# A sparse two-layer graph network on one core: node groups of 16, sums on sixteenths of the array, blocks in pairs, list comparisons on another engine

## The chip, the cores and the metric

The kernel runs on one core of a Trainium2 chip. A core has five engines with a queue of instructions each: TensorE (PE in the profile; its weight loads are listed apart as PEld), VectorE (DVE), ScalarE (ACT), GpSimd (POOL) and SyncE (SP). They work in parallel and wait for each other by semaphores. Any of them may start DMA transfers between DRAM and the on-chip memory; POOL can also start *indirect* ones, which fetch 128 rows of a table in DRAM by a list of 128 row numbers. The metric is the device time of one execution in microseconds (us), the median of several runs.

## The reference

Two graph layers, each behind a layer norm with relu and added to its input. There are 3327 nodes (padded to 3328, 26 blocks of 128) with 512 features. The adjacency matrix is sparse, and its entries fall with the product of the two nodes' numbers: the first nodes are hubs. Every node has itself as a neighbour.

```python
# layer 0
h = jnp.maximum(_layernorm(x), 0.0)
x = x + adj @ (relu(adj @ (h @ W1) + b1) @ W2) + b2          # hidden width 128
# layer 1, with the new x
h = jnp.maximum(_layernorm(x), 0.0)
type_sum = adj @ h                                           # adj_a and adj_b are the same matrix
attn_a = sigmoid(concat([type_sum, h]) @ Wa.T + ba)          # one number per node
attn_b = sigmoid(concat([type_sum, h]) @ Wb.T + bb)
hW = h @ W_sa
scores = (hW @ a_sa[:D])[:, None] + (hW @ a_sa[D:])[None, :]
e = where(adj != 0, exp(-leaky_relu(scores, 0.01)), 0.0)
x_a = (e / (e.sum(1) + 1e-5)) @ hW
x_b = adj @ (h @ W_gcnb) + b_gcnb
x = x + sigmoid(attn_a * x_a + attn_b * x_b)
```

In layer 1 the kernel first sums rows of h (once with the entries of adj, once with those of e) and multiplies with the weights afterwards.

## The kernel before

The adjacency lies transposed in DRAM (`adjT`, row = neighbour j, column = target node). `chunks` are 512 target columns; `back` is their order in the first product, from the last one to the first, which has 256.

*First product.* For each chunk PE adds up `acc_u` (L568) over 26 tiles of 128 neighbours, while DVE reduces the same tiles to `most` (L572): the largest magnitude in each group of `GW` = 32 target columns, so four groups to a block. From that `make_lists` (L433) writes, per group, the list of neighbours that have any entry in it. It works one chunk behind: `flag` says whether neighbour j touches a group, a scan counts them along j (`upto`), two small products on PE count across the partitions (`offset`), and then each list place is filled by comparison: DVE compares the place number with `offset` (L502, tile `at`), PE multiplies `at` with the counts (`p_list`, L513), DVE counts again (`past`, `jb`) and writes two tables of row numbers: `row_h` (which row of h) and `row_a` (which group of 32 entries of adjT). The generator is advanced by one step per tile of the next chunk. As soon as a list stands, POOL gathers its adjacency groups into `ae` (`gather_behind`, L216, one gather behind three of four products). Lists have room for `rooms[i]` columns of 64 places for each of the four groups; ten blocks (`OWN`) take their own 128 nodes by a plain load instead (`load_own`, L196, on ACT's queue).

*Second product.* `acc_g` (L825) is dense for the first 18 blocks of targets. The last two chunks, blocks 18 to 25, are summed by lists: POOL gathers rows of g, PE adds them up (`list_sums`, L784). `make_h1` (L639) makes the rows of layer 1, stores them to `h_dram`, and makes the logits that a node's own row gives (`own_logits`, L628; three blocks named in `LATE` and the blocks in `OWN` have them later). Block 0, the hubs, is dense in layer 1 too (`acc_hub`, L709).

*Gathered part.* Blocks 25 down to 1 are done by lists. `attend` (L917) gathers a block's rows of h into a ring of 16 tiles with two rows per partition (`pairs`), then DVE and ACT make e from the scores next to the adjacency entries in `ae`. `sums` (L968) multiplies (L981) on quarters of the array: 64 neighbours x (32 entries of adj and 32 of e) with 64 x 512 of the rows, into half of one of two PSUM banks. `copy_out` (L1052) takes the banks to `ty` on ACT, `turn` (L988) transposes (`ptt`, L995; copies `tyT`, L1010), and `weigh` (L1026) multiplies with the weights (`p_b`, L1035; `p_a`, L1042); `finish` (L875) does the rest and stores.

What sets the order: instructions of an engine run in the order of issue, and `queued` puts an instruction behind a named one of its engine. In each turn of the loop block i's scores are made, block i+2 is weighed, block i+1 turned, and block i's sums come last. POOL's order is the order in which the loop asks for gathers; `AE_PER` adjacency gathers of later blocks are asked for per block (`fetch_ae`, L912). The first gather of a block waits (`pace`, L208) until the sums of an earlier block have been done: `LEAD` = 3 blocks back for the last eight blocks, 4 for the others.

```python
    lead = LEAD[i < NB - 8]
    if k0 + k + q == extra[i] and len(combined) >= lead:
        pace(gathered[0], combined[-lead])
```

Of the kernel before, what the change touches and what calls it, by code (L numbers as in the profile page):

```python
# [9 lines left out]
F32 = mybir.dt.float32  # L10
# [10 lines left out]
GW = 32  # L21
NQ = P // GW
HALF = P // 2
ROW = 520
LEAD = 3, 4
# [13 lines left out]
LATE = 10, 11, 16  # L39

OWN = 1, 6, 7, 8, 12, 13, 14, 15, 17, 18


def list_rooms(n_blocks):

    rooms = [0, 8, 7, 6, 5, 5] + 6 * [4]
    return (rooms + n_blocks * [3])[:n_blocks]
# [3 lines left out]
def kernel(  # L51
# [35 lines left out]
    rooms = list_rooms(NB)  # L87
    extra = [int(i in OWN) for i in range(NB)]
    first = [2 * sum(rooms[:i]) for i in range(NB)]
    NL = 2 * sum(rooms)  # L90


# [21 lines left out]
    for _ in range(WAKE):  # L114
# [21 lines left out]
    ae = [  # L136
        kept([P, 2 * (r + extra[i]), 2 * GW], f"ae{i}") if r else None for i, r in enumerate(rooms)
    ]

    def segments(i):  # L140

        r = rooms[i] + extra[i]
        n = -(-r // SEG)
        cuts = [-(-r * k // n) for k in range(n + 1)]
        return list(zip(cuts, cuts[1:]))
    hubp = ctx.enter_context(tc.tile_pool(name="hubp", bufs=6))
# [26 lines left out]
    listed, fetched = set(), [0] * NB  # L173

    def gather_adj():

        order = []
        for n, (c0, w) in enumerate(back):
            order += range(c0 // P, (c0 + w) // P)[:: 1 if n < LISTED else -1]
        for i in order:  # L180
            if not i:
                continue
            r = rooms[i]
            for k0, k1 in segments(i):
                for q in range(2):
                    for k in range(max(k0, extra[i]), k1):
                        while (i, q) not in listed:
                            yield None
                        f = first[i] + q * r + k - extra[i]
                        fetched[i] += 1  # L190
                        yield gather(
                            ae[i][:, 2 * k0 + q * (k1 - k0) + k - k0, :GW], adj_groups,
                            row_a[:, f : f + 1], NP * NG - 1,
                        )

    def load_own(i):  # L196

        n = segments(i)[0][1]
        for h in range(2):
            rows = slice(i * P + h * HALF, i * P + (h + 1) * HALF)  # L200
            nc.scalar.dma_start(
                ae[i][h * HALF : (h + 1) * HALF, 0 : n + 1 : n, :GW],
                adjT[rows, rows].rearrange("j (q i) -> j q i", i=GW),
            )
# [54 lines left out]
    with (  # L259
# [109 lines left out]
        lower = kept0([P, 1], "lower", F32)  # L369
        place_row = kept0([P, max(rooms) * HALF], "place_row", F16)  # L370
# [3 lines left out]
        def make_constants():  # L374
# [4 lines left out]
            for h in range(2):  # L379
                nc.vector.memset(apart[h * HALF : (h + 1) * HALF, 2 * h : 2 * h + 2], 0.0)  # L380
# [6 lines left out]
            for t, op, base in ((before, ALU.is_gt, 0), (shift, ALU.is_equal, -1)):  # L387
# [7 lines left out]
            nc.vector.memset(lower, 1.0)  # L395
            nc.gpsimd.affine_select(
                lower, lower, pattern=[[0, 1]], compare_op=ALU.is_ge, fill=0.0, base=-HALF,
                channel_multiplier=1,
            )
            first_iota = nc.gpsimd.iota(  # L400
                place_row, pattern=[[1, max(rooms) * HALF]], base=0, channel_multiplier=0,
# [9 lines left out]
            for r in sorted(set(rooms[1:])):  # L411
                i0, n = rooms.index(r), rooms.count(r)
                cols = slice(first[i0], first[i0] + n * 2 * r)
                nc.gpsimd.memset(limit[:, NQ * i0 : NQ * (i0 + n)], float(r * HALF))
                nc.gpsimd.iota(
                    place_col[:, cols], pattern=[[0, 2 * n], [HALF, r]], base=0,
# [3 lines left out]
                    group_col[:, cols], pattern=[[NQ, n], [1, 2], [0, r]], base=NQ * i0,  # L420
# [3 lines left out]
            for t, by in ((place_col, -float(HALF)), (group_col, 2.0)):  # L424
                nc.vector.scalar_tensor_tensor(
                    t, lower.to_broadcast([P, NL]), by, t, op0=ALU.mult, op1=ALU.add
                )
            yield
            for t in ae[1:]:
                nc.gpsimd.memset(t[:, :, :GW], 0.0)  # L430
            behind.close()

        def make_lists(nth, most):  # L433
# [10 lines left out]
            for b in range(w // P):  # L444
                if extra[c0 // P + b]:
                    groups = slice(b * NQ, (b + 1) * NQ)
                    own = flag[:, groups, c0 // P + b]
                    nc.vector.tensor_tensor(own, own, apart, ALU.mult)
# [19 lines left out]
            nc.vector.tensor_copy(offset[:, :n], p_off[:, :n])  # L468
# [4 lines left out]

            step = steps[nth % 2]
            p_sh = bank(psB, f"p_sh_{c0}")
            nc.tensor.matmul(
                p_sh[:, : n * NB], shift, after[:, :n, :].rearrange(flat), start=True, stop=True
            )
            nc.vector.tensor_tensor(
                step[:, :n, :NB], p_sh[:, : n * NB].rearrange("p (b j) -> p b j", j=NB),  # L480
                upto[:, :n, :], ALU.add,
            )
            yield
            batches = []
            for i in range(c0 // P, (c0 + w) // P):
                for q in range(2 if rooms[i] else 0):
# [835 lines left out]
```

## Time and profile before

| what | us |
|---|---|
| median of three runs | 836.75 (829.47 and 842.9) |
| the profiled execution | 834.5 |
| its span | 832.8 |
| PE busy in the span | 735.6 |
| DVE busy | 506.0 |
| POOL busy | 461.1 |
| ACT busy | 194.5 |
| mean granted clock of PE | 0.94 |

Durations of single instructions come from the profiled execution; its span is the time from its first to its last instruction on the core, 1.7 less than what it was timed at. Busy times are sums over the span; the stages of this kernel use the engines in very different shares, so the windows of the span tell more than these sums. An entry such as `hr<-h_rows,row_h` names the tile written and the tiles read; buffer numbers are left out.

### The profile page before, as it was taken

Reading aid. Unit: us, or ns where it says so; the run is one execution under the profiler, and the core shown is the slowest. Engines: PE = TensorE matmul, PEld = TensorE weight load, DVE = VectorE, ACT = ScalarE, POOL = GpSimd, SP = SyncE. Lnnn points to the kernel's source line nnn. Section 1 sums busy time; section 2 is a strip of 40 time slices with the busy share of each in tenths; the row PEclk is TensorE's granted clock in tenths of the full one; section 3 lists DMA queues with packets and bytes.
Section 4 is the critical chain, followed back from the end, with each engine's and each line's share of the span. In section 5 each row is a group of like instructions: output and inputs, shape, how many; then the busy total and the mean of one; then the engine's idle time right before and its main releaser. Section 6 shows DMA issues by size and latency. Waiting matters only on the chain.

```text
span 832.8 us, 11907 instructions
## 1 busy us (share of the span) xinstructions
PE 735.6 (88%) x3595; PEld 404.5 (49%) x3595; DVE 506.0 (61%) x1625; ACT 194.5 (23%) x402; POOL 461.1 (55%) x490
## 2 busy tenths in 40 slices
PE   9999888989899771999899749967999999999995
PEld 7774333444543220444355236633656655665554
DVE  7778868898860611798987225523665557553552
ACT  7770000000000110354544002211212222221121
POOL 2201756766657776534456766674657666767500
PEclk9999989999999875999999969996999999999999
DMA  8788988988878844789994755664667877767510
GB/s 271 245 287 259 326 246 242 293 272 246 232 232 284 262 132 134 240 279 312 327 314 135 241 150 145 199 185 115 195 211 244 255 206 233 240 205 234 178 51 29
DMA packets 104889, 185.08 MB, mean 222 GB/s; under 512 B 18401, under 2 KB 35441, under 8 KB 104818
## 3 DMA queue, kind: packets, MB, share of 16 engines
q1 hardware_dynamic: 66544, 113.43, 41.8%
q0 software_dynamic: 23264, 57.64, 24.3%
q10 hardware_dynamic: 15010, 13.18, 4.9%
q8 instruction: 30, 0.49, 0.2%
q14 instruction: 41, 0.34, 0.1%
HBM read 162.29 MB, written 22.26 MB: 222 GB/s over the span
## 4 chain that ended last, share of the span: by engine, by line
PE 72%; DVE 7%; issue 6%; another core or an unknown queue 6%; DMA 5%; ACT 2%; POOL 1%; SPq 1%; DVEq 0%; ACTq 0%; POOLq 0%
PE acc_u L568 17%; PE acc L981 12%; PE p_b L1035 11%; PE p_a L1042 10%; PE acc_g L825 8%; PE pu L333 3%; PE ptt L995 3%; DMA a<-in_adjT_dram 2%; PE acc_hub L709 2%; PE px L663 2%; PE pt L325 1%; DMA xb<-in_x_dram 1%; PE acc_s L784 1%; DMA hr<-h_rows,row_h 1%
## 5 line engine op out<-in xcount | busy, mean ns | idle before, releaser
L166 POOL DMA_INDIRECT ae<-in_adjT_dram,row_a x194 | 202.6, 1044 | 181.8 <-DVE past L519 54.3
L568 PE MATMUL acc_u<-a,rows 128*128 128x512 f32 (+1 forms) x364 | 161.0, 583 | 0.5 <-DMA a<-in_adjT_dram 0.5
L166 POOL DMA_INDIRECT hr<-h_rows,row_h x120 | 122.7, 1022 | 62.5 <-issue 27.4
L825 PE MATMUL acc_g<-a,g 128*128 128x512 f32 (+1 forms) x260 | 117.1, 584 | 7.2 <-DMA a<-in_adjT_dram 6.8
L572 DVE TENSOR_REDUCE most<-a 128x16 f32<-128x512 f32 (+1 forms) x182 | 112.3, 638 | 11.6 <-issue 6.3
L1035 PE MATMUL p_b<-W_g_sb,tyT 128*128 128x257 f32 x416 | 99.3, 391 | 15.8 <-DVE tyT L1010 15.3
L1035 PEld LDWEIGHTS p_b<-W_g_sb,tyT 128*128 128x128 f32 x416 | 77.8, 192 | 46.5 <-DVE tyT L1010 15.6
L166 POOL DMA_INDIRECT rows<-h_rows,row_h x74 | 75.1, 1015 | 44.3 <-PE acc L981 20.9
L568 PEld LDWEIGHTS acc_u<-a,rows 128*128 128x128 f32 x364 | 67.2, 195 | 58.8 <-issue 56.0
L1042 PE MATMUL p_a<-W_sa_sb,tyT 128*128 128x512 f32 (+2 forms) x216 | 94.2, 577 | 0.2
L1010 DVE COPY tyT<-ptt 128x512 f32<-128x512 f32 x51 | 34.8, 685 | 87.0 <-PE p_a L1042 31.7
L825 PEld LDWEIGHTS acc_g<-a,g 128*128 128x128 f32 x260 | 50.0, 200 | 58.5 <-issue 44.9
L981 PE MATMUL acc<-hr,ae 64*64 64x512 f32 x480 | 68.3, 614 | 4.4 <-issue 4.0
L166 POOL DMA_INDIRECT g_row<-g_rows,row_h x48 | 49.0, 1021 | 20.9 <-issue 13.4
L1042 PEld LDWEIGHTS p_a<-W_sa_sb,tyT 128*128 128x128 f32 x216 | 40.7, 189 | 38.8 <-issue 36.9
L884 ACT ACTIVATE f<-f 128x2 f32<-128x2 f32 x26 | 5.3, 203 | 192.4 <-DVE f L883 97.2
L981 PEld LDWEIGHTS acc<-hr,ae 64*64 64x64 f32 x480 | 27.6, 136 | 33.6 <-issue 33.0
L343 ACT ACTIVATE gT<-acc_u,b_col 128x512 f32<-128x512 f32 (+1 forms) x7 | 4.6, 656 | 163.8 <-DMA a<-in_adjT_dram 90.9
L663 PE MATMUL px<-W_sb,sT 128*128 128x512 f32 x52 | 26.7, 650 | 15.4 <-ACT sT L799 12.0
L666 DVE TENSOR_TENSOR xb<-px,xb 128x512 f32<-128x512 f32 x26 | 17.3, 682 | 36.6 <-PE px L663 28.5
L981 PE MATMUL acc<-rows,ae 64*64 64x512 f32 x296 | 37.1, 593 | 2.5 <-issue 2.3
L623 DVE SCALAR_TENSOR_TENSOR junk<-rows,w_rows 128x512 bf16<-128x512 f32 x52 | 35.6, 684 | 3.2 <-ACT rows L244 1.1
(159 smaller groups left out, 945.2 us busy)
## 6 DMA issues: line engine op xcount, KB each, us to landing
a<-in_adjT_dram SPq DMA_DIRECT2D x286, 256.0 KB
h_rows<-rows SPq DMA_DIRECT2D x26, 260.0 KB
x<-in_x_dram SPq DMA_DIRECT2D x26, 256.0 KB
xb<-in_x_dram SPq DMA_DIRECT2D x26, 256.0 KB
x<-xb ACTq DMA_DIRECT2D x26, 256.0 KB
x1b<-x SPq DMA_DIRECT2D x26, 256.0 KB
out_dram<-va SPq DMA_DIRECT2D x25, 256.0 KB
ae<-in_adjT_dram,row_a POOLq DMA_INDIRECT x194
```

The costliest lines, as they stand in the source:

```text
L166: return nc.gpsimd.indirect_dma_start(out=dst, out_offset=None, in_=table, in_offset=bass.IndirectOffsetOnAxis(ap=rows, axis=0), bounds_ch ...
L333: nc.tensor.matmul(pu[:, :HID], hT[:, k, :], W1_sb[:, k, :], start=(k == 0), stop=(k == KD - 1))
L568: added = nc.tensor.matmul(acc[:, :w], u[j], a[:, :w], start=(j == 0), stop=(j == NB - 1))
L572: nc.vector.tensor_reduce(most[:, : w // GW, j], a[:, :w].rearrange("p (b i) -> p b i", i=GW), axis=AX.X, op=ALU.max, apply_absolute_value ...
L623: return nc.vector.scalar_tensor_tensor(junk, h, 1.0, w_rows[:, s, :], op0=ALU.mult, op1=ALU.mult, accum_out=into)
L663: last_row[2] = nc.tensor.matmul(px, sT[:, b * P : (b + 1) * P], W2_sb, start=True, stop=True)
L825: added = nc.tensor.matmul(acc[:, :w], g[j], a[:, n % per, :], start=(n == 0), stop=(n == NB - 1))
L981: added = nc.tensor.matmul(taken[i]["acc"][h][q * HALF : (q + 1) * HALF, :], both[half_p, q * n + k, :], taken[i][k0][k][half_p, q, :D], s ...
L995: moved = nc.tensor.transpose(pt[:, k * P : (k + 1) * P], ty[h][:, k * P : (k + 1) * P], ident)
L1010: last = nc.vector.tensor_copy(dst, src)
L1035: nc.tensor.matmul(p_b[n][:, :WH], tyT[:, k, 0, :], W_g_sb[:, k, n * WH : (n + 1) * WH], start=(k == 0), stop=(k == KD - 1),)
L1042: last = nc.tensor.matmul(p_a[:, c0:c1], tyT[:, k, 1, :], W_sa_sb[:, k, c0:c1], start=(k == 0), stop=(k == KD - 1),)
```

## The change

- Groups have 16 target columns instead of 32 (`GW`), eight to a block. A list of a group is shorter, and there are twice as many lists.
- Blocks are worked on in teams: block 1 alone, then (2, 3), (4, 5) up to (24, 25). A list column now has 128 places: 32 for each of the two blocks' two halves (64 for block 1's halves). Columns per team, times four for the groups: 5, 7, 5, 5, 4, 4, 4, 4, 3, 3, 3, 3, 3.
- `sums` multiplies on tiles of 32 x 32 (64 x 32 for block 1), 16 of them, into four banks.
- Each pair team takes both blocks' own nodes by plain loads: eight loads per team on ACT's queue for the adjacency, four per team on SP's for the rows of h; for the two listed chunks also loads of g. `OWN` is gone.
- The comparisons of `at` are ScalarE activations: a sigmoid with slope 200, which is 0 or 1 at whole numbers.
- `list_sums` copies the adjacency groups to block-diagonal tiles (`diag`, 16 copies on ACT), so that one product serves two halves of a block.
- The loop weighs two blocks per turn, with a turn of the next pair put between `p_b` and `p_a` of the second. `LEAD` is 2 teams. Own logits of nine blocks (`LATE`) are made in the gathered part, of all the others in `make_h1`.

```diff
-GW = 32
+GW = 16
-LEAD = 3, 4
+LEAD = 2
+STEEP = 200.0
-LATE = 10, 11, 16
-OWN = 1, 6, 7, 8, 12, 13, 14, 15, 17, 18
+LATE = 8, 10, 11, 12, 13, 14, 15, 16, 17
+def make_teams(n_blocks):
+    teams = [(1,)] + [(i, i + 1) for i in range(2, n_blocks, 2)]
+    rooms = [5, 7, 5, 5, 4, 4, 4, 4] + n_blocks * [3]
+    return teams, rooms[: len(teams)]
...
+    tall = [P // (2 * len(t)) for t in teams]
+    extra = [len(t) - 1 for t in teams]
+    def tiles_of(m):
+        return [
+            (slice(r * tall[m], (r + 1) * tall[m]), teams[m][r // 2], r % 2)
+            for r in range(P // tall[m])
+        ]
...
+    def load_own(m):
+        n = segments(m)[0][1]
+        for part, i, h in tiles_of(m):
+            for s in range(2):
+                nodes = own_rows(i, h, s)
+                nc.scalar.dma_start(
+                    ae[m][part, 2 * s * n : (2 * s + 1) * n + 1 : n, :GW],
+                    adjT[nodes, nodes].rearrange("j (q i) -> j q i", i=GW),
+                )
...
-                        nc.vector.tensor_scalar(
-                            at[:, k : k + r, h, :],
-                            place_row[:, : r * HALF].rearrange("p (k m) -> p k m", m=HALF),
-                            offset[:, b : b + 1], None, op0=ALU.is_ge,
+                    for part, i, h in tiles_of(m):
+                        b = group(i, h, q)
+                        nc.scalar.activation(
+                            at[:, k : k + r, part],
+                            place_row[:, : r * t].rearrange("p (k m) -> p k m", m=t),
+                            AF.Sigmoid, bias=offset[:, b : b + 1], scale=STEEP,
...
+                for m in teams_in(c0, w):
+                    if extra[m]:
+                        load_own(m)
...
+        def make_diag(ms):
+            for t, m in zip(diag, ms):
+                n = 4 * (rooms[m] + 1)
+                for part, i, h in tiles_of(m):
+                    nc.scalar.copy(t[part, :n, h * GW : (h + 1) * GW], ae[m][part, :, :GW])
...
-                    lead = LEAD[i < NB - 8]
-                    if k0 + k + q == extra[i] and len(combined) >= lead:
-                        pace(gathered[0], combined[-lead])
+                        if k0 + k + q == extra[m] and len(combined) >= LEAD:
+                            pace(gathered[0], combined[-LEAD])
...
             for k in range(n):
-                for q in range(2):
-                    for h in range(2):
-                        half_p = slice(h * HALF, (h + 1) * HALF)
+                for q in range(4):
+                    for r, (part, i, h) in enumerate(tiles_of(m)):
                         added = nc.tensor.matmul(
-                            taken[i]["acc"][h][q * HALF : (q + 1) * HALF, :],
-                            both[half_p, q * n + k, :], taken[i][k0][k][half_p, q, :D],
+                            taken[m]["acc"][r][q * QW : (q + 1) * QW, :],
+                            both[part, q * n + k, :], taken[m][k0][k][q][part, :D],
...
+        def next_turn(added):
+            i, ty, es = turning.pop(0)
+            with queued(added):
+                tyT, added, copied = turn(i, ty, False)
+            turned.append((i, tyT, es))
+            held.append(copied)
+            return added
...
+        def weigh_all(added):
+            while weighing:
+                final = len(weighing) == 1
+                added, end = weigh_one(added, next_turn if final and turning else None)
+                if turning:
+                    added = next_turn(added)
+                held.extend(end())
+            return added
+        for m in range(M - 1, 0, -1):
+            with queued(*held):
+                for seg in segments(m):
+                    made = attend(m, seg)
...
+            fetch_ae(2 * AE_PER)
+            held, turned = [], []
+            added = weigh_all(added)
             with queued(added):
-                for seg in segments(i):
-                    added = sums(i, seg)
+                for seg in segments(m):
+                    added = sums(m, seg)
             combined.append(added)
+            weighing = turned
+            turning, last = copy_team(m)
+            held.append(last)
```

## The prediction

> **What bounds the kernel now.** I read the page's first and fourth parts first.
>
> ```profile
> PE 735.6 (88%) x3595; PEld 404.5 (49%) x3595; DVE 506.0 (61%) x1625; ACT 194.5 (23%) x402; POOL 461.1 (55%) x490
> PE 72%; DVE 7%; issue 6%; another core or an unknown queue 6%; DMA 5%; ACT 2%; POOL 1%; SPq 1%; DVEq 0%; ACTq 0%; POOLq 0%
> ```
>
> TensorE looks like the bound and POOL half idle. That is an average over unlike stages, so next the windows: columns are the window, its length, busy us and count of PE, PEld, DVE, ACT, POOL, then granted clock, DMA share, GB/s.
>
> ```profile
> 0.00:63.00 63.00, 61.36 (x387) 47.99 (x388) 47.24 (x161) 46.40 (x105) 11.69 (x54) 1.00 0.82 267
> 63.00:235.00 172.00, 154.29 (x730) 74.67 (x729) 145.06 (x381) 4.86 (x8) 103.64 (x101) 0.95 0.86 261
> 235.00:452.00 217.00, 179.35 (x642) 82.89 (x642) 130.12 (x427) 64.93 (x114) 126.02 (x119) 0.90 0.75 243
> 452.00:577.00 125.00, 95.87 (x431) 51.56 (x430) 47.30 (x172) 19.89 (x47) 80.73 (x81) 0.86 0.59 177
> 577.00:757.00 180.00, 178.87 (x1034) 108.40 (x1034) 100.46 (x356) 42.69 (x94) 118.41 (x116) 1.00 0.73 223
> 757.00:832.80 75.80, 65.91 (x375) 38.99 (x374) 35.88 (x132) 15.75 (x36) 20.64 (x20) 0.97 0.35 110
> ```
>
> Row 1 is the normalization, row 2 the first adjacency product with the lists (DVE 145 of 172 is close behind PE), row 3 the second product, the hub and the rows of layer 1. From 452 to the end runs the gathered part, the one that the change rewrites. In row 5 PE never stops; row 4, the same work, is 29 us short of busy. The chain of waits shows one block of row 5:
>
> ```profile
> 597.04 3.49 PE acc L981 x30
> 600.53 3.67 PE p_b L1035 x16
> 604.20 3.43 PE p_a L1042 x8
> ```
>
> Block after block is 11.67 us: p_b 3.67, p_a 3.43, 1.1 for turn and small sums, and the sums of gathered rows (3.43 where a block has four columns). So PE sets the pace there. But POOL is not far: its timeline shows what a gather costs and what its pauses are.
>
> ```profile
> 538.89 1.00 POOL L166 DMA_INDIRECT hr<-h_rows,row_h  x1 [1.72 <-remote]
> 540.19 1.02 POOL L166 DMA_INDIRECT hr<-h_rows,row_h  x1 [0.30 <-issue]
> ...
> 568.93 0.99 POOL L166 DMA_INDIRECT ae<-in_adjT_dram,row_a  x1 [0.30 <-issue]
> 577.46 0.99 POOL L166 DMA_INDIRECT rows<-h_rows,row_h  x1 [7.54 <-PE acc L981]
> ```
>
> 1.00 busy and 0.30 to the next: one gather per 1.31 us at best, whatever it fetches. From 538.9 to 570.2 stand 24 without pause. In windows of one block's length:
>
> ```profile
> 538.80:550.60 11.80, 11.80 (x64) 7.20 (x63) 5.46 (x19) 2.67 (x6) 9.07 (x9) 1.00 0.66 197
> 550.60:562.40 11.80, 5.07 (x18) 2.15 (x16) 0.36 (x1) 1.34 (x3) 8.97 (x9) 0.86 0.67 188
> 562.40:574.20 11.80, 7.00 (x16) 1.75 (x19) 1.33 (x4) 0.00 (x0) 5.98 (x6) 0.50 0.43 119
> 577.40:589.20 11.80, 11.80 (x70) 7.22 (x70) 6.67 (x26) 2.18 (x7) 7.98 (x8) 1.00 0.59 183
> ```
>
> PE, DVE and ACT fall silent in the middle of the train and wake about 2 us after it. It isn't data: a copy of finished sums waits.
>
> ```profile
> 547.97 0.63 ACT L898 ACTIVATE va<-vb 128x512 f32<-128x512 f32 x1 [0.82 <-issue]
> 557.39 0.58 ACT L1054 COPY ty<-acc 128x512 f32<-128x512 f32 x1 [8.79 <-remote]
> ```
>
> Its sums had ended on PE at 546.9. Five trains have 12 gathers or more (90.5, 248.6, 302.4, 455.6, 538.9 us); in them PE, beyond its usual spacing, loses 3.9, 8.4, 21.6, 17.6 and 10.4 us. About thirty shorter ones (up to 9) lose 2 or nothing. So a long train without pause goes with a stop of the rest. The trace shows no cause, only that it starts with a dense burst of PE instructions inside the train.
>
> **The change, part by part.**
>
> *Sums.* Before: 428 matmuls of 64x64, two passes each, 856. How many run at once is read from the weight loads:
>
> ```profile
> 586.02 0.24 PEld L981 LDWEIGHTS acc<-hr,ae 64*64 64x64 f32 x4 [0.19 <-issue]
> 586.45 0.24 PEld L981 LDWEIGHTS acc<-hr,ae 64*64 64x64 f32 x4 [0.19 <-issue]
> ```
>
> Four per 0.43 us, 107 ns each: 856 x 0.107 = 92 us. After: 960 of 32x32 and 40 of 64x32 (block 1). If sixteen run at once: 1920/16 x 0.43 = 51.5, plus 80/8 x 0.43 = 4.3, 56 us: 36 us less PE. If only eight: 107, 15 more. Nearest row: p_list's 64-wide pairs are issued at 16 ns per load-and-matmul, under the 27 that sixteen per 0.43 need, so I take sixteen.
> The Trainium skill, "TensorE: Matmul & The Clock Gate", "Measured speedup vs the span model", gives 10.6 times for sixteen 32x32 tiles. The trace has four quarters at the full four times and no sixteenth. By the page the sums would take an estimated 26 us more than I count.
>
> *Gathers.* With groups of 16, lists are shorter but twice as many. POOL's order holds, from the first layer-1 gather on, 194 + 22 = 216 gathers before and 212 + 41 = 253 after (adjacency gathers 194 to 212, own-block columns not counted). 253 x 1.31 = 331 us, in a stage whose gathers now end at 785 (785 - 452 = 333). Per team of two blocks in the middle (three columns, 12 + 4 gathers) 21.0 us of POOL against 14.2 weighing + 2.3 turning + 3.4 sums = 19.9 of PE; with four columns 26.2 against 20.8; five 31.4 against 21.6; team 1 has 29 gathers, 38. **POOL becomes the bound of this stage.** PE's 36 us are then worth nothing: they become idle time of PE.
>
> *Pauses.* One gate per team (LEAD = 2) replaces one per block. The first 30 gathers come without one, then trains of 16 to 29, and, POOL being late, the gate is open when it gets there: no pause. Every train is of the long kind, and each team's sums are one burst of 128 matmuls. The rows for that are the five trains above. A burst inside a train either goes on (0) or waits for its end; I take the second, as four of the five lost 8 us or more. Then POOL and the burst take turns, since the next-but-one train is gated by the burst. Behind the gated gather on POOL's queue stand all later gathers, the adjacency ones of teams still ahead too; sums of the next team wait for them.
>
> *Banks.* A team's sums want four banks, the ones that its predecessors' turns just used. The second turn is put between p_b and p_a of a weighing, so its two copies (0.69 each) lie beside 3.43 of p_a: nothing. Without that cover 1.4 per team, 17 in all; the four copies of the sums (0.57 each) lie beside the next weighing.
>
> *List making.* 100 comparisons on DVE (L502, 300 ns at the common 128x192) go, -27 us there; scan, flag, step on twice the elements give back about 2.6 per chunk, 18. 200 ACT instructions at 0.3 (e_hub's exp, 128x128, 305 ns) = 60 us over six chunks on an engine that is idle in row 2 (4.86 of 172). PE gains 420 p_list matmuls at 16 ns, 7 us, and about 30 more switches between acc_u and p_list at about 0.1 to 0.2 (522 and 533 ns steps against 429): +9 to 11 on PE, 154 of 172 busy. Ahead of the comparisons on ACT's queue stand 16 loads of own blocks per chunk (96 in all, 20 before, 0.35 to 0.67 us each); once, at 96.57 to 104.07, an ACT issue was 7 us late. Between -10 (DVE was the wait) and +30 (each of six chunks 5 late); I take +8.
> *The rest.* Four blocks' own logits move from the gathered part into row 3 (+6.7 us of DVE, not always the bound there), and three from the lists' blocks; the train at 302 becomes 12 + 12, at best -20; 16 block copies and one or two more table loads (1.28 each) on ACT; SP's 48 small loads of own rows instead of 10 large ones, issued a team (over 20 us) ahead of their use. Between -25 and +10, I take -3. Sum ahead of 452: **+5**.
>
> **The sum**, against the profiled execution (span 832.8, 834.5 with what lies around it; the median of three runs is 836.75, within 0.3%). Gathered part: start 452; 30 gathers 39; sums of team 12 3.4; 203 gathers up to team 1's last 266; eleven bursts 41 (56 less 4.3, 3.4 and 6.9); twelve hand-overs at 0.5, 6; sums of team 1 6.9: 814. Tail: weigh 4 and 5 14.2, turn 2.2, sums 2.6, weigh 2 and 3 14.4, last sums 1.7, and from there as now (815.4 to 832.8) 17.4: 53. 867 + 5 = 872 of span, 874 in all: about 4.5% slower. Ten us up or down is the ring of 16 row pairs (a gather waiting for its tile) and the burst's length: own range 852 to 895.
>
> **Rivals.**
> 1. *Not slower: the long train doesn't stop the burst.* Then only POOL's count decides: 452 + 233 x 1.31 = 757, 13 for landing, scores and team 1's sums, 53: 823 + 5 + 2 = **830** (815 to 850). For it: trains of 8 lose nothing, and nothing in the trace names the cause. Against: five of five long ones lost. It decides if PE's bursts pass at 0.43 us per sixteen inside a train of 16; then the changed kernel's page shows PE busy through the trains.
> 2. *Slower still: sixteenths run eight at once.* In the turn-taking sum 48 of 51 us count: **922**. Speaks for it: weight loads as many as matmuls; against: the 16 ns above.
> 3. *Lists late*: the ACT queue holds p_list by 5 us per chunk; **900**.
> 4. *Faster: long trains are harmless now in the first 452 us as well* (21.6 of the train at 302, or all 34 of three): 830 - 20 to -35: **795 to 812**.
>
> **Chances.** Forecast 0.42, rival 1 0.28 (a sixth of it under 820), rival 2 0.10, rival 3 0.08, rival 4 0.12. A change under 2% (820 to 853) can't be told from none. Faster 0.12 + 0.05 = 0.17; same 0.23 of rival 1 and 0.03 of the forecast, 0.26; slower 0.57. The range leaves out half of rival 4 and most of rival 2: 812 to 915.
>
> **What would show it.** POOL about 1.31 us apart without pause from 460 to 800; PE busy in that stretch near 70%; `acc` weight loads sixteen per 0.43 us, not eight; waits of ACT's copies put down to a remote releaser all along. Wrong if POOL pauses before each team (then PE or a gate is the bound), if PE runs through trains (830), or if row 2 is over 185 us long (lists).

## The result, and the profile after

The changed kernel takes **1027.16 us** (median of four runs, 1025.52 to 1031.59) against 839.83 (four runs, 829.47 to 843.69): **1.234 times as long, interval 1.222 to 1.245**. The forecast was 874, its range 812 to 915: the sign was right, the size far off. The profiled execution took 1031.59 (span 1029.9), 197 us of span more than before.

The page's first part and the shares of the chain of waits, changed kernel:

```profile
PE 835.3 (81%) x5221; PEld 419.6 (41%) x5221; DVE 499.8 (49%) x1541; ACT 262.8 (26%) x625; POOL 499.4 (48%) x510
PE 54%; issue 11%; DVE 10%; another core or an unknown queue 10%; DMA 7%; ACT 3%; POOL 2%; ACTq 1%; SPq 1%; POOLq 0%; DVEq 0%
```

By busy time nothing explains 197 us: POOL has 38 us more, ACT 68 on an engine that is three quarters idle, DVE 6 less, and PE's 100 more hold pieces in which it was being stopped or ran at half its clock, as the views below show. PE's share of the chain fell from 72% to 54%; "issue" and "unknown queue", time in which the profile names nothing that was waited for, went from 12% to 21%. The windows say where (window, length, busy us and count of PE, PEld, DVE, ACT, POOL, granted clock, DMA share, GB/s):

```profile
0.00:65.00 65.00, 63.33 (x392) 49.55 (x393) 49.75 (x175) 46.66 (x106) 8.34 (x38) 1.00 0.81 263
65.00:266.00 201.00, 162.93 (x939) 69.05 (x938) 141.43 (x304) 56.12 (x181) 102.29 (x97) 0.90 0.75 220
266.00:494.00 228.00, 187.28 (x892) 84.50 (x893) 130.00 (x440) 81.72 (x169) 124.33 (x115) 0.86 0.73 228
511.00:971.00 460.00, 358.28 (x2705) 179.50 (x2706) 144.08 (x506) 60.81 (x128) 254.81 (x252) 0.83 0.58 162
971.00:1029.90 58.90, 46.46 (x263) 29.46 (x252) 21.14 (x69) 11.56 (x26) 0.00 (x0) 0.93 0.11 38
```

Row 2, the first product with the lists, is 201 us for 172. The gathered part is the fourth row, without its first 5.5 us (the first row gather is at 505.5): PE's 358 us are not its bound, and POOL's 252 gathers at 1.31 are 330 of its 460. Nobody is full. PE's busy share there, 78%, isn't far from the forecast's "near 70%", and would tell little; what the forecast missed is seen on POOL's own timeline:

```profile
706.93 1.00 POOL L178 DMA_INDIRECT ae<-in_adjT_dram,row_a  x1 [0.30 <-issue]
720.16 0.99 POOL L178 DMA_INDIRECT rows<-h_rows,row_h  x1 [12.22 <-PE acc L1050]
744.93 1.00 POOL L178 DMA_INDIRECT ae<-in_adjT_dram,row_a  x1 [0.30 <-issue]
758.13 1.00 POOL L178 DMA_INDIRECT hr<-h_rows,row_h  x1 [12.20 <-PE acc L1050]
```

A train of 20 gathers from 720.16 to 745.9 without pause, then 12.2 us of waiting for sums on PE, then the next. The vector engine in the same time:

```profile
732.00 0.75 DVE L962 SCALAR_TENSOR_TENSOR vb<-vb,r,va 128x512 f32<-128x512 f32 x1 [0.81 <-ACT va L961]
745.87 0.43 DVE L957 TENSOR_TENSOR vb<-p_b,bg_row 128x257 f32<-128x257 f32 x1 [13.12 <-issue]
748.70 1.29 DVE L1079 COPY tyT<-ptt 128x512 f32<-128x512 f32 x2 [1.80 <-remote]
```

It works until 12.6 us after the train's start, is silent for 13.1 us with nothing to wait for ("issue"), and starts again as the train ends. (Over all blocks the page puts most of this instruction's wait down to "remote", a releaser that it doesn't know; its row is below.) PE's timeline closes the circle:

```profile
736.03 1.04 PE L1050 MATMUL acc<-h_own,ae 32*32 32x512 f32 x3
737.37 0.58 PE L1050 MATMUL acc<-h_own,ae 32*32 32x512 f32 x1 [0.30 <-issue]
749.44 1.74 PE L1050 MATMUL acc<-h_own,ae 32*32 32x512 f32 x14 [11.49 <-DVE tyT L1079]
750.99 4.14 PE L1050 MATMUL acc<-hr,ae 32*32 32x512 f32 x49
757.68 0.48 PE L1104 MATMUL p_b<-W_g_sb,tyT 128*128 128x257 f32 x1
```

The sums don't read `tyT`. What they wait for is a place to write: the four banks of `acc` are those in which the turns put `ptt`, and a bank is free once DVE has copied its `ptt` to `tyT`. Two sums (four passes) go into the two banks that the first turn left; the third waits for the second turn's copies, which DVE left undone in its silence. The first copy ends at 749.4, the sums go on at 749.44, 3.5 us after the train, and are done at 757.7; the gate opens, and POOL goes on at 758.1. Most of the burst runs at half the clock:

```profile
749.40:755.00 5.60, 5.56 (x96) 2.82 (x99) 4.26 (x23) 1.02 (x3) 0.00 (x0) 0.50 0.10 31
755.00:757.70 2.70, 2.70 (x87) 1.52 (x58) 0.69 (x1) 0.50 (x1) 0.00 (x0) 1.00 0.23 86
```

After the 11.5 us without work PE's granted clock is 0.50, and a pass takes 1.05 us; from 755 on it is 1.00, and a pass takes 0.59. A cycle is a train and a turn one after the other: 31 us for 16 gathers (21 of train, 10 of waiting), 38 for 20 (26 and 12). The page's costliest groups and POOL's waits agree:

```profile
L178 POOL DMA_INDIRECT hr<-h_rows,row_h x140 | 141.8, 1013 | 125.2 <-PE acc L1050 76.0
L1050 PE MATMUL acc<-h_own,ae 32*32 32x512 f32 x384 | 42.0, 901 | 85.4 <-DVE tyT L1079 66.3
L957 DVE TENSOR_TENSOR vb<-p_b,bg_row 128x257 f32<-128x257 f32 x26 | 11.1, 426 | 86.4 <-remote 61.3
```
```profile
POOL hr L178 <- PE acc L1050: 76.0, 11, 12.2
POOL rows L178 <- PE acc L1050: 49.4, 7, 12.2
```

POOL waits 125 us for sums, in 18 waits, the longest 12.2; the sums wait 66 us for the copies. In before, all of POOL's waits of that part came to 45 us, in 23 gaps.

### The profile page after: what moved, and what is told of

It reads as the page before. It is cut to its first block, busy times and chain, and to the rows that moved or that the text cites. A ratio compares the mean times of both kernels' runs of the same rounds, so it can differ in the third digit from the quotient of the medians.

```text
span 1029.9 us, 15553 instructions
## 1 busy us (share of the span) xinstructions
PE 835.3 (81%) x5221; PEld 419.6 (41%) x5221; DVE 499.8 (49%) x1541; ACT 262.8 (26%) x625; POOL 499.4 (48%) x510
## 4 chain that ended last, share of the span: by engine, by line
PE 54%; issue 11%; DVE 10%; another core or an unknown queue 10%; DMA 7%; ACT 3%; POOL 2%; ACTq 1%; SPq 1%; POOLq 0%; DVEq 0%
PE acc L1050 16%; PE acc_g L891 9%; PE acc_u L607 9%; PE p_b L1104 5%; PE p_a L1112 4%; DMA a<-in_adjT_dram 4%; PE px L710 2%; PE pu L348 2%; PE acc_hub L763 2%; POOL hr L178 2%; DVE most L611 2%; DVE tyT L1079 2%; PE ptt L1064 1%; PE p_list L542 1%
## 5 line engine op out<-in xcount | busy, mean ns | idle before, releaser
L178 POOL DMA_INDIRECT ae<-in_adjT_dram,row_a x212 | 227.4, 1072 | 226.7 <-PE acc_u L607 84.7
L178 POOL DMA_INDIRECT hr<-h_rows,row_h x140 | 141.8, 1013 | 125.2 <-PE acc L1050 76.0
L607 PE MATMUL acc_u<-a,rows 128*128 128x512 f32 (+1 forms) x364 | 178.6, 613 | 5.7 <-issue 2.8
L611 DVE TENSOR_REDUCE most<-a 128x32 f32<-128x512 f32 (+1 forms) x182 | 112.9, 641 | 55.5 <-DMA a<-in_adjT_dram 34.4
L1050 PE MATMUL acc<-hr,ae 32*32 32x512 f32 (+1 forms) x1040 | 106.7, 801 | 12.2 <-issue 11.6
L1050 PE MATMUL acc<-h_own,ae 32*32 32x512 f32 x384 | 42.0, 901 | 85.4 <-DVE tyT L1079 66.3
L1104 PEld LDWEIGHTS p_b<-W_g_sb,tyT 128*128 128x128 f32 x416 | 80.1, 198 | 26.2 <-issue 10.4
L531 ACT ACTIVATE at<-place_row,offset 128x96 bf16<-128x96 f16 (+4 forms) x200 | 60.6, 393 | 117.5 <-DMA a<-in_adjT_dram 51.3
L1050 PE MATMUL acc<-rows,ae 32*32 32x512 f32 x576 | 65.1, 807 | 3.5 <-issue 3.0
L1050 PEld LDWEIGHTS acc<-hr,ae 32*32 32x32 f32 (+1 forms) x1040 | 34.1, 120 | 69.8 <-issue 66.0
L957 DVE TENSOR_TENSOR vb<-p_b,bg_row 128x257 f32<-128x257 f32 x26 | 11.1, 426 | 86.4 <-remote 61.3
```

The lines of the kernel that those rows point to most:

```text
L178: return nc.gpsimd.indirect_dma_start(out=dst, out_offset=None, in_=table, in_offset=bass.IndirectOffsetOnAxis(ap=rows, axis=0), bounds_ch ...
L531: nc.scalar.activation(at[:, k : k + r, part], place_row[:, : r * t].rearrange("p (k m) -> p k m", m=t), AF.Sigmoid, bias=offset[:, b : b ...
L607: added = nc.tensor.matmul(acc[:, :w], u[j], a[:, :w], start=(j == 0), stop=(j == NB - 1))
L611: nc.vector.tensor_reduce(most[:, : w // GW, j], a[:, :w].rearrange("p (b i) -> p b i", i=GW), axis=AX.X, op=ALU.max, apply_absolute_value ...
L1050: added = nc.tensor.matmul(taken[m]["acc"][r][q * QW : (q + 1) * QW, :], both[part, q * n + k, :], taken[m][k0][k][q][part, :D], start=(k0 ...
L1104: last = nc.tensor.matmul(p_b[n][:, :WH], tyT[:, k, 0, :], W_g_sb[:, k, n * WH : (n + 1) * WH], start=(k == 0), stop=(k == KD - 1),)
```

## The experiments

The theory **A**: a train of gathers without a pause stops the other engines, and they take turns with POOL. In its closer form **A2**, a train lets only so many instructions of the other engines start, so dense bursts meet the stop early and sparse work hardly. Rivals: POOL's count of gathers alone; the gate is set too near; the lists or the comparisons on ScalarE are late; the sums themselves are slow on sixteenths.

The kernels were run in five groups on four chips (two groups shared one), each with runs of before on the same chip: 838.52, 832.78, 838.24 and 836.99 us, but 732.45 in one group; comparisons stay within a group, or among the four whose before agrees within 1%. The changed kernel, run again in two of these, took 1031.62 (1.229, interval 1.219 to 1.240) and 1031.57; before run as a kernel of its own took 840.62 beside its 838.52.

### More instructions in every block, or longer ones

Into before, between the two halves of each block's weighing, go either 60 matmuls that are short or 6 that take about as long together.

```diff
+            for _ in range(60):                      # b_tiny60, b_tiny60_c
+                nc.tensor.matmul(p_b[0][:HALF, 300:327], dull, dull[:, :27], start=True, stop=True)
+            for _ in range(6):                       # b_long6, b_long6_c
+                nc.tensor.matmul(p_b[0][:, 300:428], ident, ident, start=True, stop=True)
```

> The kernel before, with 60 tiny bf16 matmuls (64 columns of ones times 27) between p_b and p_a of every block's weighing; their result is used by nothing. They are 120 more instruction records per block and about 1.5 us of PE. Theory A1 (what counts is how long POOL gathers without pause): only PE's own time, 25 x 1.5: 865 to 885 us. Theory A2 (what counts is how many instructions the other engines start while POOL gathers; in all long trains of both kernels that number stops near 200 to 230, whatever the train's length): each block now has some 290 in its train of 8 gathers, so the steady stretch from 577 to 757 us stalls in every block: 920 to 1050 us.

> Beside the run with 60 tiny matmuls: the kernel before with 6 matmuls of 128x128 by 128 columns (f32, about 1.4 us of PE, 24 records per block) at the same place, used by nothing. A1 and A2 both: PE's own time alone, 860 to 880 us. The difference between this and the run with tiny ones is what the number of instructions costs.

> The kernel before with 60 tiny matmuls per block, once more: in the group where the kernel before took 732 it cost 57 us and brought no stall. Where the kernel before stalls (838 in the group): A1, only the length of a train counts: 880 to 910. A2, the number of instructions started while POOL gathers counts: the steady trains of 8 stall in every block, 960 to 1100.

> The kernel before with 6 longer matmuls per block: where it cost 35 us without stalls, A1 and A2 both give 860 to 885 if the kernel before takes 838 in this group, 768 if it takes 732.

On a chip where before takes 832.78: short ones **1011.6**, long ones **857.5**, each run once like that before; +179 and +25 us. The window 577 to 757, in which before's PE never stops, first with the short, then with the long ones:

```profile
577.00:757.00 180.00, 150.46 (x1134) 91.16 (x1133) 60.37 (x208) 25.06 (x54) 73.26 (x73) 0.83 0.43 132
```
```profile
577.00:757.00 180.00, 179.58 (x1108) 116.36 (x1110) 94.38 (x332) 39.31 (x87) 109.00 (x105) 1.00 0.68 206
```

With the long ones PE is full at clock 1.00 and POOL makes 105 gathers; with the short ones POOL makes 73 and DVE 208 instructions for 332. The trains of this window are of six or eight gathers in both, but for one of 16 at its start with the short ones. How the short ones go through (PE's timeline; a train runs from 707.8 to 717.9):

```profile
711.05 1.56 PE L1042 MATMUL p_b<-dull 128*64 128x27 bf16 x44
712.81 0.17 PE L1042 MATMUL p_b<-dull 128*64 128x27 bf16 x1 [0.20 <-issue]
713.53 0.26 PE L1042 MATMUL p_b<-dull 128*64 128x27 bf16 x3 [0.54 <-issue]
716.40 0.30 PE L1042 MATMUL p_b<-dull 128*64 128x27 bf16 x3 [1.06 <-issue]
717.84 0.33 PE L1042 MATMUL p_b<-dull 128*64 128x27 bf16 x3 [0.53 <-issue]
```

The first 44 pass at 35 ns each; 5 us after the train's start, when 127 starts had gone through (117 of them PE's, matmuls and weight loads), PE drips: one to four at a time, about 0.7 us or its multiples apart. **So it is not the time that PE is busy inside a train, it is how many instructions it starts, and how densely**: a train of only eight gathers stops PE if these are dense, while before's own trains of eight let up to 168 starts pass in 10 us. That speaks for A2. PE's own starts are held here with nothing to wait for, so it isn't VectorE alone that stops.

The other chip (before 732.45): short ones 789.3, long ones 767.7, +57 and +35. There the 60 pass in one piece, although a train of six gathers stands beside them (537.7 to 545.4):

```profile
540.96 2.07 PE L1042 MATMUL p_b<-dull 128*64 128x27 bf16 x60
```

2.07 us in each of some 26 blocks make 54 of the 57: their plain PE time. With the long ones, POOL makes 106 gathers there without a pause (398.0 to 539.8), and PE is busy 139 of these 142 us:

```profile
398.00:539.80 141.80, 139.10 (x773) 87.07 (x771) 68.13 (x235) 28.30 (x62) 109.77 (x106) 0.99 0.71 212
```

**That chip doesn't stop.** The five stops that the prediction listed, 62 us, would be the largest part of the 100 us between the chips; no trace of before itself was kept there.

### A pause after every eighth gather

```diff
+        if train[0] % 8 == 0:                        # a_pause8, b_pause8, in gather()
+            with queued(g):
+                for _ in range(12):
+                    train[1] = nc.gpsimd.memset(idle, 0)
```

> The changed kernel, with POOL kept from gathering for about 2 us after every eighth gather (twelve small memsets on POOL). Theory A (a long run of gathers without pause holds up the other engines from about its twelfth microsecond on, and a pause ends it): the stretches of 9 to 13 us in which PE, DVE and ACT stand still in each of about eleven trains of the gathered part go, though POOL has some 60 pauses of 2 us more to make: 900 to 960 us against 1027. Theory B (POOL's number of gathers, or the gate two teams back, sets the time): the pauses come on top, 1060 to 1150 us. Theory C (the 32x32 sums themselves are what is slow): within 2% of 1027.

> The kernel before, with the same pause of about 2 us on POOL after every eighth gather. Theory A: the five long trains lose their stalls (62 us of PE time beyond its usual spacing) and pay for pauses of some 20 us in them; elsewhere POOL had pauses anyway: 780 to 810 us against 837. Theory B (POOL's count or the data is what those stretches wait for): 840 to 890 us.

These ran on the chip that doesn't stop, beside 732.45: 967.6 and 881.7 (1.206, 1.200 to 1.212). A pause came out as 3.4 us, so eight gathers cost 13.8 instead of 10.4, and 59 and 54 such pauses are added to POOL's time. They say nothing for or against A; what they do give is the time of a team's sums with nothing in their way, in the changed kernel with pauses: 4.6 to 4.9 us for 128 passes (three bursts, from 569 to 631), at a granted clock of 1.00.

```diff
+        if train[0] > 219 and train[1] >= 8:         # a_split8: in the gathered part alone;
+            train[1] = 0                             # train[1] starts at 1 with each team's gate
+            with queued(g):
+                for _ in range(7):
+                    train[2] = nc.gpsimd.memset(idle, 0)
```

> The changed kernel with a pause of some 2 us on POOL (seven small memsets) after the eighth and sixteenth gather of each team's train, in the gathered part alone. If a pause clears the stop: a team no longer stands still for the 9 to 13 us from about its tenth gather to the train's end, and pays 2 to 4 for the pauses; its sums can begin beside the second half: 900 to 970 where the changed kernel takes 1030. If the stop is only POOL's count, or a pause doesn't clear it: 1030 to 1070.

**989.1** on a chip where before is 836.99: some 42 us better than the changed kernel elsewhere, less than hoped. The pauses (1.79 to 2.0 us) work: POOL's waits for sums fall from 125 to 31 us. But the sums now lie inside the second piece of the train:

```profile
682.53 0.28 PE L1101 MATMUL p_b<-ones,es 32*64 32x1 f32 x4
682.74 1.14 PE L1063 MATMUL acc<-h_own,ae 32*32 32x512 f32 x32
683.62 4.71 PE L1063 MATMUL acc<-rows,ae 32*32 32x512 f32 x31
689.18 1.06 PE L1063 MATMUL acc<-hr,ae 32*32 32x512 f32 x3 [0.35 <-issue]
690.63 1.06 PE L1063 MATMUL acc<-hr,ae 32*32 32x512 f32 x4 [0.39 <-issue]
692.07 8.18 PE L1063 MATMUL acc<-hr,ae 32*32 32x512 f32 x86 [0.37 <-issue]
```
```profile
690.99 1.79 POOL L193 MEMSET idle<- 128x128 uint8 x7
```

The first 32 pass in 0.88 us (682.74 to 683.62), sixteen per 0.44: sixteenths do run sixteen at once. The next 31 take 5 us and then three or four at a time every 1.45 us, until POOL's second pause (691.0). The whole is 17.4 us for what the forecast had at 4.3. Here PE itself is stopped, with nothing that the trace shows to wait for.

### Fewer gathers

The changed kernel with only the lists of groups 0 and 1 of each block gathered; groups 2 and 3 use the rows of 0 and 1, so half the row gathers are left out and the sums are of the wrong rows.

```diff
-                    two = [next(pairs) for _ in range(2)]
+                    two = 2 * [next(pairs)]
-                    for q in range(4):
+                    for q in range(2):
```

> The changed kernel with every second gather of rows of h left out (groups 2 and 3 use the rows of groups 0 and 1), so that its output is not the reference's; sums, weighing and all instructions of the other engines stay. POOL has 147 gathers in the gathered part in place of 253, a team's train is 8 to 14 long in place of 16 to 24. If the trains are what the stop needs: most of each team's 12 to 15 us go, 840 to 900 where the changed kernel takes 1030. If the sums alone were slow: 1000 to 1030.

**880.3** (before 838.24). PE's instructions are all there, the trains behind the first are 10 to 15 long, and POOL's waits behind them are shorter:

```profile
597.32 1.00 POOL L178 DMA_INDIRECT rows<-h_rows,row_h  x1 [8.54 <-PE acc L1050]
621.50 1.00 POOL L178 DMA_INDIRECT hr<-h_rows,row_h  x1 [8.86 <-PE acc L1050]
```

Cycles of 21 to 26 us, still a train and a turn in sequence. 106 gathers fewer are 139 us of POOL by count; about 150 went, of a loss of some 190. All the sums were left in: it is the gathers that carry the loss, and 42 us stay. But POOL still waits 108 us for sums, where it waited 125; most of what went is the time of the gathers themselves, so this run doesn't tell a stop from POOL's count.

### The gate's place, and the comparisons

```diff
-LEAD = 2
+LEAD = 3                                             # a_lead3
-                        nc.scalar.activation(        # a_dve: as before, offset from p_off
-                            ... AF.Sigmoid, bias=offset[:, b : b + 1], scale=STEEP,
+                        nc.vector.tensor_scalar(
+                            ... offset[:, b : b + 1], None, op0=ALU.is_ge,
```

> The changed kernel with the gate three teams back in place of two (LEAD = 3). If POOL's wait for the sums two teams back (about 12 us in each team) is a cost of its own, POOL starts each team's gathers earlier: 30 to 100 us less than the changed kernel in this group. If the gathers' own count or the stall is what counts: within 2% of it, or slower for longer trains.

> The changed kernel with the list comparisons back on VectorE (200 comparisons as tensor_scalar), all else as changed. If ScalarE's comparisons, behind the many small loads on its queue, are what made the first product 35 us longer: 20 to 35 us less than the changed kernel in this group. If the longer trains of gathers and the 808 list products are: within 10 us of it, or up to 30 slower, as DVE (143 of 201 us busy there) gets 50 us more work.

Beside 1031.6: **1046.0** with the gate a team further back, **1015.3** with the comparisons on VectorE again. Both are single runs and within 2%. A gate further back lets the gathers go earlier, but then every team's sums lie inside a train (12 to 35 us a burst) and POOL still waits 110 us for them. So the gate's place isn't the cause. Taking the comparisons back ends the first product at 253.4 instead of 265.9 (the changed kernel again, on the same chip): 12.5 us of the 16. Among what ScalarE's comparisons waited for the trace names loads, though not which of these waits cost time; changed kernel:

```profile
ACT at L531 <- DMA a<-in_adjT_dram: 51.3, 2, 36.8
ACT at L531 <- DMA ae<-in_adjT_dram: 29.4, 2, 14.9
```

### Fewer, wider sums

The sums on 64x64 tiles, two neighbouring groups' columns together: 500 matmuls for 1000. They mix neighbouring groups, so what they compute is not the reference.

```diff
-                for q in range(4):
+                for q in (0, 2):
...
-                            both[part, q * n + k, :], taken[m][k0][k][q][part, :D],
+                            cols, taken[m][k0][k][q][wide, :D],
```

> The changed kernel with its sums on 64x64 tiles in place of 32x32: each product takes two neighbouring groups and 64 neighbours, so there are half as many (500 for 1000) and the four banks are filled as before; the sums then mix groups, so the output is not the reference's. By the 107 ns per 64x64 pass of the kernel before, TensorE needs 6.9 us for a team of four columns, where the 32x32 sums take 6.2 when nothing disturbs them. If the number of instructions started beside the gathers is what costs (0.05 us each by the run with 60 tiny matmuls), 128 fewer records per team and 12 teams: 930 to 980 where the changed kernel takes 1030. If only the gathers' count or the gate costs: 1025 to 1045.

**1047.6** (before 838.24): no gain, a miss for A2 as far as the sums go. After a stop their bursts took 9.5 to 11.5 us for 60 to 76 passes, one 13.7. In the trains from 579 to 829 VectorE stops as before, with four passes of the sums through and 166 to 172 starts in the train, where the changed kernel has 167 to 173: the stop comes before the sums, so their number could hardly matter there.

### The gate in before, and three attempts to gain

```diff
-                    if k0 + k + q == extra[i] and len(combined) >= lead:
+                    if i % 2 == 0 and k0 + k + q == extra[i] and len(combined) >= lead:   # b_gate2
-LEAD = 3, 4
+LEAD = 3, 3                                          # b_lead3, b_fix, b_fix2
```

b_fix adds a pause of 7 memsets after every sixth gather up to the 244th; b_fix2 only two, after the 8th and the 16th of the first 24 gathers of the gathered part.

> The kernel before with the gate only at every second block's first gather, so that the steady trains of 8 gathers become trains of 16; the gathers themselves, the sums and all else are as before. Where the kernel before takes 838: each pair of blocks meets one long train and loses 8 to 12 us in it, 11 times: 920 to 970 (both A1 and A2). Where it takes 732: within 10 us of it.

> The kernel before with LEAD = 3 for all blocks: the one ungated stretch of 24 (or 16 and 16) gathers where the gate goes from three blocks back to four is gone. Where the kernel before takes 838: 10 to 20 us less, since that train's stall of 10 to 19 us goes. Where it takes 732: within 5 us.

> The kernel before with LEAD = 3 for all blocks and a pause of some 2 us on POOL (seven small memsets) after every sixth gather up to the 244th, so that no train of the first two products or of the gathered part's start starts more than about 130 instructions without a pause. Where the kernel before takes 838, if a pause clears what has piled up: 770 to 810. If such pauses don't clear it, or POOL is late by them (40 pauses, 80 us, in some 400 us that it is 60% busy): 835 to 870.

> The kernel before with LEAD = 3 for all blocks and a pause of some 2 us after the eighth and sixteenth of the 24 gathers that begin the gathered part (its longest train, in which PE loses some 17 us), and nowhere else. If a pause clears the stop: 10 to 15 us less than the kernel before where that takes 838, so 823 to 828. If it doesn't, or if what follows waits for the gathers themselves: 833 to 845.

One gate for two blocks, before's lists and sums untouched: **870.6** against 832.78, +38. Trains of 16, 12 to 14 and 9 come of it; PE is idle 1 to 7 us in each of those of 12 to 16, and not in those of 9. The gate alone, without a sixteenth in sight, makes the kernel slower; but it is a fifth of the whole loss, less than expected.

The three attempts: 835.76 (0.9975, 0.9934 to 1.0015), 841.84 (1.0054, 1.0023 to 1.0085), 840.38 (1.0013, 0.9971 to 1.0056). No gain, three misses: where one train lost its stop, another gained one, or the pauses cost POOL's time where its gathers are the path: in b_fix the second product's last matmul ends 19 us earlier than in before's profile (425.2 for 444.2), the first row gather comes only 2 us earlier (453.2 for 455.6). No version here beats before.

## Why the prediction was wrong

The mechanism was in the main the forecast's own: POOL's trains and PE's bursts take turns, because a train stops the rest. Its sizes fell short by 158 us (872 of span against 1029.9):

| term | forecast | measured | difference, us |
|---|---|---|---|
| start of the gathered part (first row gather) | 457 | 505.5 | +48.5 |
| gathers on the path, at 1.31 | 305 (233) | 336 (255) | +31 |
| what POOL waits for between them | 50 | 127 (19 gaps) | +77 |
| from the last of them to the end of team 1's sums | 6.9 | 3.0 | -4 |
| tail | 53 | 58 | +5 |

- ***Pauses* failed, in size and in its picture: the largest term.** It wrote "POOL being late, the gate is open when it gets there", and priced a turn at the burst alone, 3.4 to 4.3 us and 0.5 of hand-over. The gate was closed 18 times; "POOL pauses before each team" was even among its own signs of being wrong. A stop leaves not only the burst undone but what stands ahead of it: 3.5 us pass from the train's end (745.9) until a copy has freed the next bank (749.4), and then the burst, at half the clock for most of its time, takes 6.8 to 7.4 us where 128 passes were to take 3.4, and 8.1 to 8.7 where 160 were to take 4.3. Behind a train of 20 that makes 12 us a turn instead of 5. The prediction had rows that pointed to a higher price and didn't use them: its five long trains had lost PE 12.4 us each on average. Eleven turns at that are 136, near the 127 measured, but that is partly luck, as the one counts PE's loss inside a train and the other POOL's wait behind it.
- **"Five of five long ones lost" was a count of trains whose gathers come at an even 1.31 us.** By POOL's pauses alone before has more trains of 12 and over, and beside one of 13 (434.6 to 452.0) PE goes on:

```profile
434.55:452.04 17.49, 17.32 (x57) 9.97 (x56) 11.81 (x39) 7.80 (x16) 13.83 (x13) 1.00 0.35 108
```

- ***Gathers*: the price of one held (1.31), the count on the path did not.** The forecast ended POOL's chain at team 1's last gather and put the last team's 20 beside other work. But team 1's sums lay among those last gathers (943.3 to 971.8 on PE) and ended only behind them (the last is at 967.8).
- ***Sums*: the width held, the price of a burst did not.** 32 passes went in 0.88 us where nothing stopped them. Rival 2, eight at once, is out. A whole burst with nothing in its way took 4.6 to 4.9 us for 128 passes, where 3.4 was forecast. After a stop a pass costs 52 to 59 ns over the burst, and the clock says why: at 0.50 sixteen go in 0.85 us, at 1.00 in 0.45 to 0.6. The Trainium skill, "TensorE: Matmul & The Clock Gate", "Measured speedup vs the span model", gives 10.6 times for sixteen small tiles; a pass of 512 columns takes 0.43 us here (eight of `p_a` in 3.43), so the undisturbed stretch is nearly 16 times, a whole undisturbed burst about 12 and a burst after a stop about 8.
- ***List making* and *The rest*: +5 was forecast, +50 came** (first row gather at 455.6 in before, 505.5 now; the sum had set 452 and 5). Of these, the first product with the normalization is 36 longer (its last matmul ends at 267.0 for 231.5), the second product 14. The comparisons on ScalarE are 12 to 16 (the run with them back on VectorE, once): the forecast named the queue and its loads, and chose +8 within its bounds of -10 and +30. The other 34 or more are only argued: ahead of the gathered part stand eight trains of 12 or more gathers where there were six, and PE is idle 57 us in them and the 2 us behind each, where it was 37. Rival 3, lists late, was right in kind at less than half its price of 5 us per chunk, and its sign, row 2 over 185 us, is there with 201; not all of that is the lists.
- ***Banks* failed with *Pauses*.** It put the second turn's two copies at nothing, as they would lie beside `p_a`. With VectorE stopped they don't: PE's sums wait 66 us for these copies (row above), in nine waits, and it is by these banks that a stop of VectorE becomes a wait of PE and then of POOL. How long the turn would be with banks to spare, no run here shows.
- **Rival 1 (830)** is out on the chips where both kernels ran: PE doesn't run through the trains. On the chip that doesn't stop it stays open: the changed kernel itself never ran there, though that is the plainest test of all of this.

Left open: what in the chip links a software gather's issue to the other engines' starts. The records name no waiter ("issue", or an unknown one), and no run here shows the resource. One rival was left untested: the recording itself. Each time here comes with a span and a granted clock that were read from records of that execution, and the stop depends on how many recorded instructions start how densely; no execution without records is there to compare, so it isn't excluded that part of the stop belongs to the recording. A plain count isn't the whole of it either: in the changed kernel's trains from 583 to 816 us, 167 to 173 starts of PE (with its weight loads), VectorE and ScalarE fall into a whole train, beside 60 short matmuls 118 to 142 pass in 5 us before the stop, and the train of 13 above lets 162 pass in 17.5 us with no stop.

## What to carry to other kernels

A train of gathers and a dense run of small instructions on another engine don't overlap on most of the chips used here, however idle each engine's share looks: look at how many instructions start beside a train, and how densely, not at busy time alone. Trains broken by pauses made the changed kernel some 42 us faster (one run, against runs on other chips) and gained nothing in before. When two engines take turns, the price of a turn is not the short burst; it is all that the stop left undone ahead of the burst (here a copy that held a bank), and the burst at the clock that it finds after the stop. So look at what a stop cost in the old trace. Groups of half the size made 255 gathers behind the first of rows where there were 216, each at 1.31 us whatever it fetches, and sums on smaller tiles didn't pay for them.

## What the runs showed of the hardware

- In the traces of the comparison and of four groups of five (three chips of four), VectorE, ScalarE and PE stop beside a train of gathers without a pause. In the changed kernel's trains of 16 and 20 from 583 to 816 us VectorE's last start is 11.7 to 12.6 us after the train's and ScalarE's 12.5 to 13.4; VectorE then starts nothing for 9.5 to 13.9 us, goes on between 3.2 us before and 1.3 us after the train's end, and makes the copy that frees a bank 2.3 to 2.8 us after it. Beside short, dense matmuls PE stops 5 us after the train's start, and its starts come about 0.7 us or multiples apart. In the train with pauses PE went on 1.1 us after the start of one of 1.8 us on POOL.
- After 11.5 us without work PE's granted clock was 0.50 for the next 5.6 us and 1.00 then; a pass of 512 columns on a sixteenth took 1.05 and 0.59 us.
- The same program took 732 us on one chip and 833 to 840 on the others; there the stop is absent (60 short matmuls in 2.07 us beside a train, and 106 gathers without a pause beside a PE busy 139 of 142 us). What sets that chip apart isn't known.
- A uint8 memset of 128x128 on POOL takes 0.26 us (7 are 1.79, 12 are 3.10), so it makes a short pause of chosen length.
